# Two layers of graph network on 32 batches: where a search, a scaling, two norms and a verdict stand in the order

## The chip, the cores and the metric

The kernel runs on one core of a Trainium2 chip. The metric is the device time of one execution in microseconds (us), lower is better: 2764.36 us, the median of three runs from 2764.18 to 2764.61.

## What is computed

The reference, cut to what matters: 32 batches of 512 rows by 512 columns, one adjacency matrix of 512 x 512, all in float32.

```python
def layer0(x):                       # H = 8 heads of HD = 64
    q, k, v = x @ Wq + bq, x @ Wk + bk, x @ Wv + bv
    scores = einsum('bihd,bjhd->bhij', q, k) / sqrt(64)
    scores = scores + where(adj == 0, -1e9, 0)
    return einsum('bhij,bjhd->bihd', softmax(scores), v)

def layer1(x):
    y = einsum('nm,bmd->bnd', adj, x)
    return einsum('bnd,do->bno', y, weight) + bias

x = layernorm(x + layer0(x))
x = layernorm(x + layer1(x))
```

## The kernel before, in words

The work of a batch goes through TensorE in these steps. `project` (L372) makes q, k and v in seven products each instead of eight (a Strassen scheme over 2 x 2 blocks, `block_product` L362; the sums of blocks are made on VectorE and GpSimd). `scores` (L558) multiplies keys by queries per head, adds the mask on VectorE (L570), takes the exponential on ScalarE (L572) and adds up the exponentials on GpSimd (L583). `attend` (L585) multiplies by the values (L592). `fold_squares` (L614) and `add_up` (L628) make the sums of the softmax, and `turn_out` (L598) turns the result of a pair of heads by 32 x 32 blocks on VectorE and has SyncE copy 16 squares into `rows`, one DMA of 16 KB each (L611). `scale_rows` (L644) divides these rows by the sums on ScalarE (eight operations L649 for a pair of heads), and `add_rows` (L651) adds them to the input on GpSimd.

Then the first norm: `statistics` (L425) of four blocks of rows on VectorE (L431, L432), `square_root` (L434) on ScalarE, `invert_root` (L437, lines L440 and L441) on VectorE, `normalise` (L444, line L446) on ScalarE. For the second layer each row is split into a high half, rounded to TensorE's fast float format, and the rest: `split` (L464, lines L457 and L461). `aggregate` (L481) multiplies both halves by the adjacency matrix (L488), and `convolve` (L527) multiplies by the weight, again in seven products, whose results are added to the input on VectorE and, by way of a tile `mix`, on GpSimd (L537 to L544). The second norm is made with `statistics`, `norm` and `normalise` again (its statistics are called `survey`), and `store` (L468) writes a batch out.

The work is laid out by hand. [...] Units of work are listed by `units_of` (L722) for each batch, in two slots of the main loop (L764): slot 0 holds the projections of the next batch, slot 1 its values, the aggregation of the batch before and the convolution of the batch before. `merge` (L715) puts the lists named `behind` after the units of TensorE one by one. So in batch 31, the last, slot 0 holds the convolution of batch 29, with the statistics (`fresh`), root and norm (`young`) and the splits of batch 30 behind its products, and slot 1 the aggregation of batch 30.

What follows the main loop is the end of the last batch (L786 to L844), in which nothing of a later batch is left to fill TensorE's waits: the convolution of batch 30 (`rest`), the first norm of batch 31, its aggregation by rows (`split_rows` L497, lines L502 and L503; `add_bias` L505; `aggregate_rows` L508, products L515, copies to `yT` L520 and L522), its convolution (`last`), and the second norms of batches 29, 30 and 31 with their stores. In the aggregation by rows the high and low tiles have two buffers each, so the third block's halves wait for the first block's products, and the fourth's for the second's.

The kernel takes two shortcuts that hold for the given kind of input, and tests them as it goes: that sums of exponentials stay finite, and whether the adjacency matrix is exact in the fast format. For the second, `look_for_low_half` (L305) rounds a block of rows on ScalarE (L308), compares it with the original on VectorE into a tile of the tag `attT` (L310), and counts the differences (L311). The tag has two buffers, which `turn_out` uses as well. `judge` (L665) makes one number per row of all tests, in seven small operations of VectorE; a last product of TensorE (L843) adds them up, and VectorE writes `verdict` (L844). After it every engine reads the verdict and branches: were it 1, a general kernel would run.

Results of TensorE lie in a ring of eight banks (`bank`, L223); a new product waits until the bank's reader of eight products ago is done.

Of the kernel before, what the change touches and what calls it, by code (L numbers as in the profile page):

```python
# [207 lines left out]
def fast_kernel(ctx: ExitStack, tc, verdict, x, adj, Wq, bq, Wk, bk, Wv, bv, W1, b1, out):  # L208
# [3 lines left out]
    HP = H // 2  # L212
    NB = N // P
    DB = D // P
    assert N == 512 and D == 512 and H * HD == D
    root = float(HD) ** 0.5

    consts = ctx.enter_context(tc.tile_pool(name="consts", bufs=1))
# [249 lines left out]
    def store(b, blocks=None):  # L468
        for c in blocks or ():
            nc.sync.dma_start(out[b, c * P:(c + 1) * P, :], X[b][:, c, :])  # L470
        if blocks is None:
            nc.sync.dma_start(out[b].rearrange("(c p) d -> p c d", p=P), X[b])
# [30 lines left out]
        nc.vector.tensor_sub(low, row, high.bitcast(FP))  # L503

    def add_bias(b, c):  # L505
        nc.vector.tensor_add(X[b][:, c, :], X[b][:, c, :], b1_r)  # L506

    def aggregate_rows(b):  # L508

        yt = YT[b] = work.tile([P, 7, 2, half], FP, name="yT", bufs=1)  # L510
        banks = [bank(2, half) for _ in range(DB)]
        for c in range(NB):
            for d, pm in enumerate(banks):
                for part in (LOW[b, c], HIGH[b, c]):
                    nc.tensor.matmul(pm.rearrange("p a n -> p (a n)"), part[:, d * P:(d + 1) * P], adjT[:, c, :],  # L515
                                     start=(c == 0 and part is LOW[b, c]), stop=(c == NB - 1 and part is HIGH[b, c]))
        for d, pm in enumerate(banks):
            block = yt[:, d // 2:d // 2 + 3:2, d % 2, :]
            if d % 2:
                nc.vector.tensor_copy(block, pm)  # L520
            else:
                nc.scalar.activation(block, pm, AF.Copy)  # L522
            if d >= 2:
                nc.vector.tensor_add(yt[:, A_AT["S1"], d % 2, :], pm[:, 1, :], yt[:, A_AT["A21"], d % 2, :])
        combine_rows(yt)

    def convolve(b, i):  # L527

        pm = bank(2, half)
        block_product(pm, YT[b], w1, i)  # L530
        x11, x12, x21, x22 = (X[b][:, 2 * r:2 * r + 2, s * half:(s + 1) * half] for r in range(2) for s in range(2))
        if i == 1:

            MIX[b] = work.tile([P, 2, half], FP, name="mix", tag="q" if b >= B - 3 else "low", bufs=2)
            nc.scalar.activation(MIX[b], pm, AF.Copy)
        if i in (6, 7):
            nc.vector.tensor_add(MIX[b], pm, MIX[b])  # L537
            for block in (x12,) if i == 6 else (x21, x22) if b == B - 1 else (x22,):
                nc.gpsimd.tensor_add(block, block, MIX[b])
        for block in {1: (x11,), 5: (x12, x22), 2: (x11,), 3: (x12,), 4: (x21,)}.get(i, ()):  # L540
            nc.vector.tensor_add(block, pm, block)  # L541
        if i == 4 and b < B - 1:

            nc.gpsimd.tensor_add(x21, x21, MIX[b])  # L544
# [6 lines left out]
    def convolution(b):  # L551
        return [(convolve, b, i) for i in (1, 2, 5, 6, 7, 3, 4)] if b >= 0 else []
# [125 lines left out]
    def run(units):  # L678
        for unit in units:
            unit[0](*unit[1:])  # L680
# [26 lines left out]
    def survey(b):  # L707

        return [(statistics, b, 1, c) for c in range(NB)] if b >= 0 else []
# [5 lines left out]
    def merge(units, behind):  # L715

        merged = []
        for k in range(max(len(units), len(behind))):
            merged += units[k:k + 1] + (behind[k] if k < len(behind) else [])
        return merged  # L720

    def units_of(b):  # L722

        made, turned = projections(b + 1), flips(b + 2)
        splits, gathered = aggregation(b - 1)
        old, seen = norm(b - 1, 1), survey(b - 2)

        fresh, young = ([(statistics, b - 1, 0, c) for c in range(NB)], norm(b - 1, 0)) if b else ([], [])
        scaled, added = residuals(b, 0)
        if b == B - 1:  # L730


            first, second = folds(b, 1)
            behind = [fresh[:2], fresh[2:], young[:1], young[1:3], young[3:5] + [first], young[5:] + splits[:1],
                      splits[1:]]
            return [merge(convolution(b - 2), behind), [second] + merge(gathered, [scaled, added, seen[:2], seen[2:]])]

        ready = [(turn_over, b)] if b > 1 else []
        if old:
            behind = [seen[:2], seen[2:], old[:2], old[2:4] + fresh[:2], old[4:] + ready + fresh[2:]] + [  # L740
                [u] for u in young]
        elif b:
            behind = [ready + fresh] + [[u] for u in young]
        else:
            behind = [[]] + [[(sum_weights, w1, n)] for n in range(4)]
        behind += [[] for _ in range(11 - len(behind))]
        behind += [splits[:1], scaled + added, splits[1:2]]
        slot0 = merge(made[:16], behind)
        values = made[16:]
        looked = [(look_for_low_half, c) for c in range(NB)] if b == 0 else []  # L750
        scaled, added = residuals(b, 1)
        slot1 = values[:3] + looked[:2] + gathered[:1] + splits[2:3] + gathered[1:2] + splits[3:] + scaled[:1]
        slot1 += values[3:] + looked[2:]
        if b == B - 2 > 0:
            slot1 += [(load, B - 1)]
        slot1 += gathered[2:3] + turned[:1] + gathered[3:]
        convolved = convolution(b - 1) if b < B - 2 else []
        slot1 += merge(convolved, [scaled[1:] + added[:1] + turned[1:2], turned[2:3], turned[3:4], [], [], [],
                                   added[1:] + turned[4:]])
        return [slot0, slot1]  # L760
# [27 lines left out]
    rest, last = convolution(t - 1), convolution(t)  # L788
    for hp in range(HP - PAIRS, HP):
        last_residual(t, hp)  # L790
    run(rest[:1])
    old, seen = norm(t - 1, 1), survey(t - 1)
    run(old[:1] + rest[1:2] + old[1:])
    if t > 1:
        store(t - 2)

    for c in range(NB):
        statistics(t, 0, c)
    ahead = norm(t, 0)
    run(ahead[:1] + rest[2:3] + ahead[1:2])  # L800
    for c in range(NB):
        run(ahead[2 + c:3 + c] + rest[3 + c:4 + c])
        split_rows(t, c)
    run(rest[3 + NB:])
    for c in range(NB):
        add_bias(t, c)
    aggregate_rows(t)


    halves = {}  # L810
# [4 lines left out]
            halves[c] = spare[:, c, :, :]  # L815
        nc.vector.bn_stats(halves[c][:, s, :], X[t][:, c, s * half:(s + 1) * half])  # L816

    old = norm(t, 1)
    beside = {1: seen, 2: old[:2], 5: old[2:3], 6: old[3:5], 7: old[5:]}
    for unit in last:  # L820
        run([unit] + beside.get(unit[2], []))
        if unit[2] == 2:
            well = judge()
        if unit[2] == 7 and t > 0:
            store(t - 1)
        for c, s in {2: ((0, 0), (1, 0)), 3: ((0, 1), (1, 1)), 4: ((2, 1), (3, 1), (2, 0), (3, 0))}.get(unit[2], ()):
            half_statistics(c, s)
            if (c < 2) == (s == 1):
                if t + 1 not in STAT:
                    for table, name, shape in ((STAT, "stat", (2 * NB, 2)), (RSTD, "rstd", (2 * NB,)),  # L830
                                               (SHIFT, "shift", (2 * NB,))):
                        table[t + 1] = work.tile([P, *shape], FP, name=name, bufs=3)
                nc.vector.bn_aggr(STAT[t + 1][:, NB + c, :], halves[c])
        ready = {3: (0, 1), 4: (2, 3)}.get(unit[2], ())
        if ready:
            slots = slice(NB + ready[0], NB + ready[1] + 1)
            square_root(t + 1, slots)
            invert_root(t + 1, slots)
            for c in ready:
                normalise(t + 1, NB + c)  # L840
                store(t, [c])
    pm = bank(N)
    nc.tensor.matmul(pm[0:1, 0:1], well, ones[:, 0:1], start=True, stop=True)  # L843
    nc.vector.tensor_scalar(verdict, pm[0:1, 0:1], P - 0.5, None, op0=ALU.is_lt)  # L844


# [22 lines left out]
```

## Time and profile before

| | |
|---|---|
| median of three runs | 2764.36 us |
| the profiled execution | 2764.78 us |
| its span, first to last instruction | 2762.9 us |
| TensorE, busy in the span | 2735.6 us, 99% |
| VectorE | 2068.2 us, 75% |
| GpSimd | 1902.6 us, 69% |
| ScalarE | 1411.1 us, 51% |
| last product of TensorE ends | 2749.9 us after the span's start |
| last store is issued | 2757.6 us |

The page names engines PE (TensorE), PEld (its weight loads), DVE (VectorE), ACT (ScalarE), POOL (GpSimd) and SP (SyncE, whose DMA issues are shown as SPq). L570 is line 570 of the kernel. A line of the waits reads: engine, line, who released it, us in total, how many times, the longest. A line of the timeline reads: start in us from the span's start, how long the group took, engine, line, operation, output <- input with sizes, count, and in brackets the engine's idle time before it and what ended that. One matmul in float32 shows as two passes, so x8 are four products. A product of 128 x 128 by 128 x 512 halves (L488, L515) is one pass.

From batch 2 on the main loop repeats every 84.9 us, TensorE without a wait.

### The profile page before, as it was taken

The page shows a single profiled execution, that of the slowest core. Times are in us where ns is not written, and L with a number is a line of the kernel's source. Part 1 is how long each engine was busy: PE and PEld are TensorE (multiplying, and loading weights), DVE is VectorE, ACT ScalarE, POOL GpSimd, SP SyncE. Part 2 cuts the span into 40 slices and gives each one's busy share as a digit, 9 for nine tenths or more (in the row PEclk, how much of TensorE's full clock was granted, in tenths as well). Part 3 has the DMA queues.
Part 4 walks back from the last instruction along what each step waited for, and adds up shares of the span by engine and source line. Part 5 has one row for each costly group of instructions (what it writes and reads, how often), then busy time and mean ns, then how long its engine had stood idle before and what let it go on. Part 6 is the DMA issues. An engine that isn't in the chain of part 4 may idle for free.

```text
span 2762.9 us, 39328 instructions
## 1 busy us (share of the span) xinstructions
PE 2735.6 (99%) x12842; PEld 1912.7 (69%) x12842; DVE 2068.2 (75%) x3347; ACT 1411.1 (51%) x2459; POOL 1902.6 (69%) x1223
## 2 busy tenths in 40 slices
PE   9999999999999999999999999999999999999997
PEld 6666766767767667677676676776766767767665
DVE  6777777787777777777777777777777777787777
ACT  2455544655545546445554465454554544655554
POOL 4666777667767667676677776776666867667774
PEclk9999999999999999999999999999999999999999
DMA  5122212222122222122221222211222212222121
GB/s 147 29 31 57 45 30 56 60 60 56 25 49 58 61 56 36 38 56 62 58 53 21 56 59 60 56 26 48 58 62 57 44 30 56 61 58 57 26 51 49
DMA packets 592915, 142.20 MB, mean 51 GB/s; under 512 B 554560, under 2 KB 558656, under 8 KB 592704
## 3 DMA queue, kind: packets, MB, share of 16 engines
q1 hardware_dynamic: 592704, 139.63, 23.1%
q8 instruction: 103, 1.69, 0.3%
q14 instruction: 108, 0.88, 0.1%
HBM read 72.88 MB, written 33.55 MB: 39 GB/s over the span
## 4 chain that ended last, share of the span: by engine, by line
PE 97%; DVE 1%; SPq 1%; ACT 0%; DMA 0%; issue 0%; POOL 0%; DVEq 0%; ACTq 0%
PE bank L369 55%; PE bank L568 16%; PE bank L592 16%; PE bank L488 8%; SPq L611 1%; PE bank L633 0%; DVE bnst L431 0%; DMA wq<-in_L_gnn_Wq_dram 0%; ACT rows L649 0%; PE bank L515 0%; DVE xT L541 0%; DVE part L816 0%; DVE xs L541 0%; DVE xT L506 0%; DVE low L503 0%
## 5 line engine op out<-in xcount | busy, mean ns | idle before, releaser
L572 ACT ACTIVATE e<-e 128x1024 f32<-128x1024 f32 x512 | 524.6, 1053 | 581.3 <-DVE e L570 559.5
L570 DVE SCALAR_TENSOR_TENSOR e<-gap,bank 128x512 f32<-128x512 uint8 x1024 | 617.9, 681 | 20.2 <-PE bank L568 20.2
L583 POOL TENSOR_TENSOR es<-es,e 128x1024 f32<-128x1024 f32 x256 | 618.2, 2415 | 20.1
L583 POOL TENSOR_TENSOR es<-e 128x1024 f32<-128x1024 f32 x128 | 315.9, 2468 | 333.0 <-ACT e L572 333.0
L568 PE MATMUL bank<-q,k 64*128 64x512 f32 x2048 | 465.2, 599 | 0.0
L592 PE MATMUL bank<-e,v 128*64 128x512 f32 x2048 | 456.5, 598 | 4.7 <-DVE v L404 4.7
L369 PE MATMUL bank<-wv,xT 128*128 128x256 f32 x1792 | 405.4, 381 | 0.0
L369 PE MATMUL bank<-xT,wk 128*128 128x256 f32 x1792 | 403.0, 379 | 0.7 <-DVE wk L319 0.7
L369 PE MATMUL bank<-xT,wq 128*128 128x256 f32 x1792 | 403.1, 383 | 0.4 <-DMA wq<-in_L_gnn_Wq_dram 0.4
L369 PE MATMUL bank<-w,yT 128*128 128x256 f32 x1792 | 392.3, 379 | 0.5 <-DVE yT L520 0.5
L568 PEld LDWEIGHTS bank<-q,k 64*128 64x128 f32 x2048 | 204.0, 186 | 259.6 <-issue 160.4
L369 PEld LDWEIGHTS bank<-w,yT 128*128 128x128 f32 x1792 | 340.0, 190 | 48.1 <-DVE yT L520 0.9
L369 PEld LDWEIGHTS bank<-xT,wk 128*128 128x128 f32 x1792 | 340.2, 190 | 47.2 <-PE bank L369 1.1
L369 PEld LDWEIGHTS bank<-xT,wq 128*128 128x128 f32 x1792 | 339.5, 191 | 47.4 <-ACT xT L344 0.8
L369 PEld LDWEIGHTS bank<-wv,xT 128*128 128x128 f32 x1792 | 337.5, 190 | 47.5 <-DVE e L570 0.8
L649 ACT ACTIVATE rows<-rows,zero,inverse 128x64 f32<-128x64 f32 x1008 | 343.2, 427 | 0.0
L592 PEld LDWEIGHTS bank<-e,v 128*64 128x64 f32 x2048 | 142.2, 137 | 283.8 <-issue 282.7
L653 POOL TENSOR_TENSOR xs<-xs,rows 128x512 f32<-128x512 f32 x124 | 158.4, 1289 | 168.0 <-DMA xs<-in_x_dram 168.0
L572 ACT ACT_TABLE_LOAD x30 | 38.5, 1283 | 423.9 <-DVE e L570 423.9
L461 DVE TENSOR_TENSOR low<-xs,high 128x512 fp32r<-128x512 f32 x122 | 143.5, 1176 | 104.2 <-ACT high L457 104.2
L446 ACT ACTIVATE xs<-xs,shift,rstd 128x512 f32<-128x512 f32 x248 | 181.9, 803 | 32.5 <-DVE shift L441 32.5
L541 DVE TENSOR_TENSOR xs<-bank,xs 128x512 f32<-128x512 f32 x186 | 124.5, 683 | 96.9 <-PE bank L369 46.5
(122 smaller groups left out, 2970.1 us busy)
## 6 DMA issues: line engine op xcount, KB each, us to landing
rows<-attT SPq DMA_DIRECT2D x2016, 16.0 KB, 1.8
xin<-in_x_dram SPq DMA_DIRECT2D x496, 64.0 KB, 2.5
xs<-in_x_dram SPq DMA_DIRECT2D x31, 1024.0 KB, 5.2
out_dram<-xs SPq DMA_DIRECT2D x31, 1024.0 KB, 4.4
xin<-in_x_dram SPq DMA_DIRECT2D x4, 256.0 KB, 3.6
wq<-in_L_gnn_Wq_dram SPq DMA_DIRECT2D x2, 512.0 KB, 6.2
wk<-in_L_gnn_Wk_dram SPq DMA_DIRECT2D x2, 512.0 KB, 8.2
yT<-in_adj_dram SPq DMA_DIRECT2D x1, 1024.0 KB, 7.9
```

The lines of the kernel that those rows point to most:

```text
L369: nc.tensor.matmul(pm[:, r, :], left[:, d, r * P:(r + 1) * P], right[:, d, :], start=(d == 0), stop=(d == 1))
L446: nc.scalar.activation(row, row, AF.Identity, bias=SHIFT[t][:, slot:slot + 1], scale=RSTD[t][:, slot:slot + 1])
L461: nc.vector.tensor_sub(LOW[b, d], cols, HIGH[b, d].bitcast(FP))
L488: nc.tensor.matmul(pm.rearrange("p a n -> p (a n)"), part, adjT[:, n % NB, :], start=(n == 0), stop=(n == 2 * NB - 1))
L541: nc.vector.tensor_add(block, pm, block)
L568: nc.tensor.matmul(ps[s], keys[:, j * P:(j + 1) * P], queries, start=True, stop=True)
L570: nc.vector.scalar_tensor_tensor(e[:, s, :], gap[:, j, :], NEG * root, ps[s], op0=ALU.mult, op1=ALU.add)
L572: nc.scalar.activation(e, e, AF.Exp, scale=1.0 / root)
L583: nc.gpsimd.tensor_add(ES[b, hp], ES[b, hp] if j > 1 else E[b, hp, 0], E[b, hp, j])
L592: nc.tensor.matmul(po[s * HD:(s + 1) * HD, :], values, e[:, s, :], start=(j == 0), stop=(j == NB - 1))
L649: nc.scalar.activation(part, part, AF.Identity, bias=zero, scale=inverse[:, c, s:s + 1])
L653: nc.gpsimd.tensor_add(cols, cols, ROWS.pop((b, hp)))
```

## The change

It moves steps and changes a few; the products of TensorE stay the same and in the same order, the verdict's excepted.

- The four searches (`look_for_low_half`) leave slot 1 of batch 0 and stand behind the eighth to eleventh products of slot 0 of batch 1.
- Slot 0 of batch 31: `scaled`, the scaling of the first two pairs of heads, stands behind the first two products of batch 29's convolution, ahead of the root of batch 30's norm; before, it stood behind the first two aggregations of slot 1. The statistics of batch 29 (`seen`) leave slot 1.
- At the end: the norm of batch 29 and the statistics of batch 30 leave the convolution of batch 30. Statistics of batch 29 and two of batch 30 are now made between that convolution's last addition and `aggregate_rows`, and the rest beside the last convolution, with both norms and stores.
- `add_bias` of batch 31 runs on GpSimd instead of VectorE.
- In the last convolution the seventh product's sum goes to a new `mix` tile instead of the one that GpSimd reads.
- `judge` stands behind the fourth product (unit 6) of the last convolution, and the verdict's product behind the fifth (unit 7), ahead of the last two; before, it was the last.
- The last norm: blocks 2 and 3 take their statistics after blocks 0 and 1 are normalised, and block 3 is normalised on VectorE.

```diff
-        nc.vector.tensor_add(X[b][:, c, :], X[b][:, c, :], b1_r)
+        nc.gpsimd.tensor_add(X[b][:, c, :], X[b][:, c, :], b1_r)
...
-            nc.vector.tensor_add(MIX[b], pm, MIX[b])
+            mixed = MIX[b]
+            if i == 7 and b == B - 1:
+                MIX[b] = work.tile([P, 2, half], FP, name="mix", tag="q", bufs=2)
+            nc.vector.tensor_add(MIX[b], pm, mixed)
...
-            behind = [fresh[:2], fresh[2:], young[:1], young[1:3], young[3:5] + [first], young[5:] + splits[:1],
-                      splits[1:]]
-            return [merge(convolution(b - 2), behind), [second] + merge(gathered, [scaled, added, seen[:2], seen[2:]])]
+            behind = [fresh[:2] + scaled[:1], fresh[2:] + scaled[1:], young[:1], young[1:3], young[3:5] + [first],
+                      young[5:] + splits[:1], splits[1:]]
+            return [merge(convolution(b - 2), behind), [second] + added + gathered]
...
             behind = [ready + fresh] + [[u] for u in young]
+            behind += [[(look_for_low_half, c)] for c in range(NB)]
...
-        looked = [(look_for_low_half, c) for c in range(NB)] if b == 0 else []
...
-        slot1 = values[:3] + looked[:2] + gathered[:1] + splits[2:3] + gathered[1:2] + splits[3:] + scaled[:1]
-        slot1 += values[3:] + looked[2:]
+        slot1 = values[:3] + gathered[:1] + splits[2:3] + gathered[1:2] + splits[3:] + scaled[:1]
+        slot1 += values[3:]
...
     run(rest[:1])
-    old, seen = norm(t - 1, 1), survey(t - 1)
-    run(old[:1] + rest[1:2] + old[1:])
-    if t > 1:
-        store(t - 2)
-
     for c in range(NB):
         statistics(t, 0, c)
     ahead = norm(t, 0)
-    run(ahead[:1] + rest[2:3] + ahead[1:2])
+    run(ahead[:1] + rest[1:2] + ahead[1:2])
     for c in range(NB):
-        run(ahead[2 + c:3 + c] + rest[3 + c:4 + c])
+        run(ahead[2 + c:3 + c])
         split_rows(t, c)
-    run(rest[3 + NB:])
+        run(rest[2 + c:3 + c])
+    run(rest[2 + NB:])
+    older, seen = survey(t - 2), survey(t - 1)
+    run(older)
     for c in range(NB):
         add_bias(t, c)
+    run(seen[:2])
     aggregate_rows(t)
+    old = norm(t - 1, 1)
...
-    old = norm(t, 1)
-    beside = {1: seen, 2: old[:2], 5: old[2:3], 6: old[3:5], 7: old[5:]}
+    next_ = norm(t, 1)
+    beside = {1: old + seen[2:3], 2: seen[3:] + next_[:2], 5: next_[2:4], 6: next_[4:]}
+    upper, lower = slice(NB, NB + 2), slice(NB + 2, 2 * NB)
     for unit in last:
         run([unit] + beside.get(unit[2], []))
+        if unit[2] == 1 and t > 1:
+            store(t - 2)
         if unit[2] == 2:
+            for c in range(2):
+                half_statistics(c, 0)
+        if unit[2] == 6:
             well = judge()
-        if unit[2] == 7 and t > 0:
-            store(t - 1)
...
+            if t > 0:
+                store(t - 1)
+        if unit[2] == 3:
+            for c in range(2):
+                half_statistics(c, 1)
+                close(c)
+            square_root(t + 1, upper)
+        if unit[2] == 7:
+            pm = bank(N)
+            nc.tensor.matmul(pm[0:1, 0:1], well, ones[:, 0:1], start=True, stop=True)
+            nc.vector.tensor_scalar(verdict, pm[0:1, 0:1], P - 0.5, None, op0=ALU.is_lt)
+    invert_root(t + 1, upper)
+    for c in range(2):
+        normalise(t + 1, NB + c)
+        store(t, [c])
+    for c in (2, 3):
+        half_statistics(c, 1)
+        half_statistics(c, 0)
+        close(c)
+    square_root(t + 1, lower)
+    invert_root(t + 1, lower)
+    normalise(t + 1, NB + 2)
+    row = X[t][:, 3, :]
+    nc.vector.tensor_scalar(row, row, STAT[t + 1][:, NB + 3, 0:1], RSTD[t + 1][:, NB + 3:NB + 4],
+                            op0=ALU.subtract, op1=ALU.mult)
+    store(t, [2, 3])
```

`half_statistics` (L813) takes the statistics of half a block's columns, `close` joins the two halves of a block. The order of the last products is 1, 2, 5, 6, 7, 3, 4.

More of the change, by code (lines that the diff above doesn't have):

```diff
@@ L214, in fast_kernel @@
     DB = D // P
-    assert N == 512 and D == 512 and H * HD == D
+    assert N == 512 and D == 512 and H * HD == D and B > 2
     root = float(HD) ** 0.5
@@ L816, in half_statistics, with close @@
         nc.vector.bn_stats(halves[c][:, s, :], X[t][:, c, s * half:(s + 1) * half])
-    old = norm(t, 1)
-    beside = {1: seen, 2: old[:2], 5: old[2:3], 6: old[3:5], 7: old[5:]}
+    def close(c):
+        nc.vector.bn_aggr(STAT[t + 1][:, NB + c, :], halves[c])
+    for table, name, shape in ((STAT, "stat", (2 * NB, 2)), (RSTD, "rstd", (2 * NB,)), (SHIFT, "shift", (2 * NB,))):
+        table[t + 1] = work.tile([P, *shape], FP, name=name, bufs=3)
+    next_ = norm(t, 1)
+    beside = {1: old + seen[2:3], 2: seen[3:] + next_[:2], 5: next_[2:4], 6: next_[4:]}
@@ L820, in fast_kernel @@
+    upper, lower = slice(NB, NB + 2), slice(NB + 2, 2 * NB)
     for unit in last:
         run([unit] + beside.get(unit[2], []))
+        if unit[2] == 1 and t > 1:
+            store(t - 2)
         if unit[2] == 2:
+            for c in range(2):
+                half_statistics(c, 0)
+        if unit[2] == 6:
             well = judge()
-        if unit[2] == 7 and t > 0:
-            store(t - 1)
[L826 to L844, printed above, removed]
+            if t > 0:
+                store(t - 1)
```

## The prediction

> **What bounds the kernel now.** I read the page first, then TensorE's waits, then the timeline of each engine where TensorE idles: early in batch 1, and in the last batch.
>
> ```profile
> span 2762.9 us, 39328 instructions
> PE 2735.6 (99%) x12842; PEld 1912.7 (69%) x12842; DVE 2068.2 (75%) x3347; ACT 1411.1 (51%) x2459; POOL 1902.6 (69%) x1223
> ```
>
> TensorE is the bound. Only its idle time, its slow clock and the tail behind its last product can change; the change leaves its products alone. The waits:
>
> ```profile
> PE bank L592 <- DVE v L404: 4.7, 1, 4.7
> PE bank L515 <- DVE low L503: 4.3, 2, 4.0
> ...
> PE bank L369 <- DVE yT L520: 0.5, 1, 0.5
> ```
>
> The change touches all three. TensorE around the first (start, duration):
>
> ```profile
> 124.40 1.94 PE L592 MATMUL bank<-e,v 128*64 128x512 f32 x8
> 131.02 8.03 PE L592 MATMUL bank<-e,v 128*64 128x512 f32 x24 [4.68 <-DVE v L404]
> 138.98 9.47 PE L568 MATMUL bank<-q,k 64*128 64x512 f32 x32
> ```
>
> VectorE in the same stretch: a search stands in a DMA wait, and the values behind it are late:
>
> ```profile
> 127.80 1.15 DVE L310 TENSOR_TENSOR attT<-yT,high 128x512 f32<-128x512 f32 x1 [4.54 <-DMA rows<-attT]
> 128.99 0.69 DVE L311 TENSOR_REDUCE inexact<-attT 128x1 f32<-128x512 f32 x1
> 129.59 1.28 DVE L404 TENSOR_TENSOR v<-bank,v 128x512 f32<-128x512 f32 x2
> 142.44 9.62 DVE L570 SCALAR_TENSOR_TENSOR e<-gap,bank 128x512 f32<-128x512 uint8 x16
> ```
>
> GpSimd meanwhile adds up the exponentials that the second fold of this stretch needs:
>
> ```profile
> 126.06 5.10 POOL L583 TENSOR_TENSOR es<-es,e 128x1024 f32<-128x1024 f32 x2
> ```
>
> In the last batch, the lines of TensorE, ScalarE and SyncE that I price from:
>
> ```profile
> 2702.58 1.20 PE L488 MATMUL bank<-adjT,low 128*128 128x512 f32 x4
> 2727.58 0.76 PE L515 MATMUL bank<-adjT,low 128*128 128x512 f32 x1 [3.96 <-DVE low L503]
> 2738.07 11.92 PE L369 MATMUL bank<-w,yT 128*128 128x256 f32 x54 [0.46 <-DVE yT L520]
> ```
> ```profile
> 2692.96 0.30 ACT L435 ACTIVATE rstd<-stat,eps 128x4 f32<-128x4 f32 x1 [3.26 <-DVE stat L432]
> 2695.49 2.93 ACT L446 ACTIVATE xs<-xs,shift,rstd 128x512 f32<-128x512 f32 x4 [2.24 <-DVE shift L441]
> 2705.24 5.42 ACT L649 ACTIVATE rows<-rows,zero,inverse 128x64 f32<-128x64 f32 x16
> ```
> ```profile
> 2676.78 21.50 SPq L611 DMA_DIRECT2D rows<-attT  x32
> ```
>
> [...] granted clock 0.50 from 131 to 136 us and from 2727.5 to 2730.5. There 24 passes took 7.96 instead of 24 x 0.2193 = 5.26 (2.7 lost), and 24 of L515 took 7.16 instead of 24 x 0.2325 (1.6 lost). [...] L503 took 0.69 alone and 1.38 beside POOL's L544.
>
> **Part 1, the searches moved to batch 1.** Removed from batch 0: four pairs L310+L311, 6.6 us (1.6+1.8+1.6+1.7, start to start), and the 4.5 us DMA wait. Without them L404 follows its last product (124.4) and ends near 125.1. Four transposes L353 take 2.4 (127.5), fold and turn of the first head pair (L623, L625, L606: 136.43 to 139.43 before) 3.0 to 3.1 (130.6). The second fold needs GpSimd's sums, done at 131.16: so 131.2, and with 3.05 its turn ends at 134.25. Then L570 starts, at 142.44 before: 8.2 earlier. Before, too, VectorE paced those scores (9.47 against 7.14 us elsewhere), so what follows on TensorE moves by the same **8.2**. Bounds: 9.9, all that this stretch loses (from one run of 128 products L369 to the next 75.18 us, where the pieces of the chain, 27.8 + 2 x (7.02 + 7.14 + 0.2) for attention and 5 x 1.74 for five value products, give 65.2), and 7.0, if the sums come a microsecond late. In the new place VectorE idles 10.4 us between 157.5 and 177.5 and gets 6.6 more; the rows that free the two attT buffers should have landed by then (estimate 155.3, search 157). ScalarE's four copies, 2.2 us, and the scaling behind them come some 6 us late, into idle time ahead of the second half of the batch. Cost 0; 1 to 2 if that cover is short. Batch 0 has no DMA of its own in this edit, and SyncE's queue keeps its order.
>
> **Part 2, scaling of the last batch in front of the square root.** Sixteen L649 now stand behind the mix (ends 2688.4), ahead of table load, L435 and L446. Their rows are issued one by one by SyncE: 32 from 2676.78, the last at 2697.7, landing 1.8 us later: 2699.5. The first eight end near 2691.4; of the second pair all but the first operation wait for the last rows: 2699.55 + 2.42 = 2702.0. In the order of the changed program the table load still stands directly before the root, so it can no longer run early. Then table 1.28, root 0.30 (2703.6), L440 and L441 (2704.0), four L446 2.93 (2707.0), L457 0.6 (2707.6), L461 0.7 (2708.3): L488 starts at 2708.4 instead of 2702.58. The change adds a wait: behind it on ScalarE stand root, norm and high halves of batch 30, on VectorE L440 and everything after, on TensorE the aggregation. **5.8** idle, plus 1.6 of slow clock (0 to 2.8): **7.4**. The 5.4 us freed later on ScalarE hide behind the aggregation.
>
> **Part 3, statistics and norm of batches 29 and 30 moved back.** Let T be the end of that aggregation. VectorE reaches the first residual product L660 at T+1.3, 4.6 us earlier against T than before, without four statistics in front. With residuals 2.7, add 0.6, own statistics 3.3, root and shift 1.0, L446 0.8, L502 0.6, L503 0.7 the first low half is there at T+11. The product itself comes free later: TensorE is done at T+13.4 (8 transposes and 12.25 of L369). The L515 wait goes: 3.96 + 1.6 + 0.3 = **-5.9**. What is late next: the yT copy. Between the last L503 and L520 now stand two adds (1.2), four statistics of batch 29 and two of batch 30 (6 x 0.8 = 4.8); the four bias adds (2.4) have gone to GpSimd, 4 x 1.27 there, done before TensorE needs them. With S the start of L515: the last L503 must wait for the second block's products, S+3.7, high half, and GpSimd's add beside it: ends S+5.75. Then 1.2, 4.8 and the copy 0.6: S+12.4. L515 ends at S+7.75, half a product follows: idle 4.15 instead of 0.46, and 0.3 for the last block: **+4.0**; slow clock +0.75 (0 to 2.8)[...].
>
> The stores of batches 29 and 30 also go later on SyncE, behind norms that end near S+19 and S+22; a store of 1 MB lands in 4.3 us, so both are out before the last four are issued (S+28 on). Cost 0.
>
> **Part 4, judge and verdict.** VectorE's order in the last products is: first add (behind the mix), L440, statistics, add, statistics, L440 (waiting for ScalarE's four L446), half statistics, two adds, mix, seven small operations 0.8. From S+12.4: yT copies and sums 1.3 beside the first product (S+14.1), mix copy 0.6, add 0.6, L440 and L441 0.4, statistics 0.8, add 0.6, statistics 0.8, then the wait until the root behind four L446 is there (S+19.0), 0.4, half statistics 0.7, adds 1.2, mix 0.6, judge 0.8. That gives S+22.8; TensorE has its first five products at S+20.8. The verdict product stands between, so it waits **+1.9** (0 to 2).
>
> **Part 5, the end.** Now 2762.9 - 2749.9 = 13.0 follow the last product: VectorE lags, since L537 stood 1.38 us behind GpSimd (the new mix tile ends this). New, from the last product's end: add 0.75, inverse and shift 0.35, statistics of blocks 2 and 3 1.85, root 0.35, inverse 0.4, L446 0.85 with block 3 on VectorE beside it, second store's issue 0.4, then 5.3 as now from the last issue to the end: 10.3. **-2.7** (-2 to -3.3).
>
> **Sum.** -8.2 + 7.4 - 5.9 + 4.0 + 0.75 + 1.9 - 2.7 = -2.75. The profiled run took 2764.78 (span 2762.9 and 1.9 around it): 2762.0. The median is 0.42 lower: **2761.6**. What a measurement can tell is 0.2%, 5.5 us: faster below 2758.8, slower above 2769.9.
>
> **Rivals.** *The rows come in time* (0.12): then part 2 costs nothing and the total is -10.2: 2754.2. For it: in batches before, the same scaling found its rows landed. Against: SyncE's 21.5 us of issue, which begins when GpSimd frees the rows' buffers at 2676.7 and which the change doesn't touch. *The searches take their price along* (0.07), the slower side: if in batch 1 the rows land later than the search, VectorE stands before it, behind it the eviction of projections. As soon as eight banks (8 x 1.74 us) don't cover the delay, TensorE waits; with the whole 8.2 back, the tail's +5.45 stays: 2769.9, and with both slow clocks at their upper ends 2773. Against: the 10.4 idle. *Slow clock and verdict at their lower ends* is inside my case: -2.75 - 1.6 - 0.75 - 1.9 = -7, 2757.4; both clocks at their upper ends give 2764.9.
>
> **How the numbers follow.** Forecast 0.81, of it 0.12 under 2758.8; rivals 0.12 and 0.07. Faster 0.24, same 0.69, slower 0.07. The forecast's own range is 2757 to 2766.5 with the bounds of parts 1 to 5; the rivals' 0.19 may stay outside.
>
> **What would show it.** Part 1: no L592 wait, batch 1's first L369 near 140.3. Part 2: L488 waits about 6 us on L461, ScalarE idle before L649. Part 3: no long L515 wait, about 4 us on L520. Part 4: a 1 to 2 us wait at the verdict. Wrong would be: scaling without a wait, or a search that waits on DMA again.

## The result, and the profile after

The changed kernel takes 2766.02 us (median of 12 runs, 2763.67 to 2767.72), the kernel before 2764.57 us (12 runs beside it, 2763.43 to 2765.93). The ratio is 1.0005, 95% interval 0.9997 to 1.0012: no difference that can be told. The forecast of 2761.6 us was 4.4 us too low. In the traces the span grew from 2762.9 to 2764.7 us, by 1.8, where the sum had said -2.75. So there are 4.55 us to find.

The page of the kernel after, its first lines (TensorE's busy time counts slow passes as busy, 5.20 of 5.20 us at a granted clock of 0.50 further down, so it says nothing about the clock):

```profile
span 2764.7 us, 39351 instructions
PE 2735.4 (99%) x12842; PEld 1915.2 (69%) x12842; DVE 2065.1 (75%) x3344; ACT 1411.5 (51%) x2458; POOL 1908.4 (69%) x1227
```

TensorE's waits of the kernel after. The L592 wait (now L596) is gone and the one of L515 is down to 0.3, as meant; three others stand there instead:

```profile
PE bank L488 <- DVE low L461: 5.7, 1, 5.7
PE bank L369 <- DVE yT L520: 4.0, 1, 4.0
PE bank L849 <- DVE well L678: 2.8, 1, 2.8
PE bank L515 <- DVE low L503: 0.3, 1, 0.3
```

TensorE at the start of batch 1, kernel after. The 32 passes of values run through, and the first projection of the batch starts at 139.42 instead of 148.57:

```profile
124.03 7.09 PE L596 MATMUL bank<-e,v 128*64 128x512 f32 x32
131.05 8.26 PE L572 MATMUL bank<-q,k 64*128 64x512 f32 x32
139.42 8.90 PE L369 MATMUL bank<-xT,wq 128*128 128x256 f32 x40
```

TensorE at the end, kernel after. In front of each of the three groups stands its wait, in brackets. Read the durations too: 38 passes that take 8.47 at full speed took 10.16, and the last 16 took 5.40 instead of 3.72 (both full-speed values are from runs shown below):

```profile
2699.97 2.05 PE L488 MATMUL bank<-adjT,low 128*128 128x512 f32 x4 [5.71 <-DVE low L461]
2735.92 10.16 PE L369 MATMUL bank<-w,yT 128*128 128x256 f32 x38 [4.00 <-DVE yT L520]
2748.91 0.19 PE L849 MATMUL bank<-ones,well 128*1 128x1 f32 x2 [2.84 <-DVE well L678]
2749.04 5.40 PE L369 MATMUL bank<-w,yT 128*128 128x256 f32 x16
```

ScalarE in front of the first of these waits. The scaling (L653) waits for its rows, and table load and root stand behind it, as priced; the last statistics that the root needs were ready at 2684.53, and it ran at 2694.77:

```profile
2685.35 0.44 ACT L653 ACTIVATE rows<-rows,zero,inverse 128x64 f32<-128x64 f32 x1 [2.69 <-DMA rows<-attT]
2691.02 2.43 ACT L653 ACTIVATE rows<-rows,zero,inverse 128x64 f32<-128x64 f32 x7 [5.24 <-DMA rows<-attT]
2693.47 1.28 ACT L435 ACT_TABLE_LOAD   x1
2694.77 0.30 ACT L435 ACTIVATE rstd<-stat,eps 128x4 f32<-128x4 f32 x1
```

VectorE, kernel after, two lines that matter below: an idle stretch of 2.45 us in front of the third block's low half, and an operation of the judge on 128 x 2 numbers that took 1.18 us:

```profile
2726.09 0.69 DVE L503 TENSOR_TENSOR low<-xT,high 128x512 fp32r<-128x512 f32 x1 [2.45 <-ACT high L502]
...
2747.20 1.18 DVE L675 TENSOR_SCALAR well<-seen 128x2 f32<-128x2 f32 x1
```

GpSimd at that moment, kernel after, and the same operation of the judge in the kernel before (there L671):

```profile
2747.09 1.26 POOL L543 TENSOR_TENSOR xT<-xT,mix 128x512 f32<-128x512 f32 x1 [6.11 <-DVE mix L541]
```
```profile
2745.24 0.17 DVE L671 TENSOR_SCALAR well<-seen 128x2 f32<-128x2 f32 x1
```

The granted clock of TensorE, kernel after, in stretches behind the three waits (from:to, length, busy time of TensorE with its instructions, granted clock, share of the DMA engines, GB/s). Each wait is followed by a stretch at half speed:

```profile
2700.00:2705.20 5.20, 5.20 (x12) 0.50 0.00 0
2705.60:2707.00 1.40, 1.40 (x8) 1.00 0.00 0
2735.95:2736.15 0.20, 0.20 (x1) 1.00 0.00 0
2736.40:2739.40 3.00, 3.00 (x9) 0.50 0.00 0
2749.00:2749.70 0.70, 0.70 (x5) 1.00 1.03 389
2750.00:2753.10 3.10, 3.10 (x8) 0.50 0.44 161
```

Where the time went, step by step (after minus before, from the two timelines of TensorE; they add up to the 1.8 of the spans):

| step | predicted | in the traces |
|---|---|---|
| head: to batch 1's first projection | -8.2 | -9.15, of it 0.37 a lead from the first loads, ahead of anything that was changed |
| rest of the main loop | 0 | +0.8, of it 0.5 behind the searches |
| wait of L488 | +5.8 | +5.71 |
| its slow clock | +1.6 | +2.47 |
| aggregation's end to end of L515 | -5.9 | -5.55 |
| wait for the yT copy | +4.0 | +3.54 |
| its slow clock | +0.75 | +1.69 |
| wait for the verdict, with the product | +1.9 | +2.96 |
| its slow clock | not priced | +1.68 |
| last convolution in two pieces instead of one run | not priced | +0.33 |
| behind the last product | -2.7 | -2.71 |

The two later clock rows compare the same passes slow and at full speed (10.16 with 8.47, 5.40 with 3.72). The row of +0.33 is what is left: the two pieces at full speed take 12.19 us together, where the kernel before has one run of 11.92. Of the 4.55 us, 3.5 are slow clock (5.84 instead of 2.35), 1.06 is the verdict and 0.33 the two pieces; the other steps take back about 0.35.

### The profile page after: what moved, and what is told of

The parts are those of the page before. It is cut to its first block, busy times and chain, and to the rows that moved or that the text cites. A ratio compares the mean times of both kernels' runs of the same rounds, so it can differ in the third digit from the quotient of the medians.

```text
span 2764.7 us, 39351 instructions
## 1 busy us (share of the span) xinstructions
PE 2735.4 (99%) x12842; PEld 1915.2 (69%) x12842; DVE 2065.1 (75%) x3344; ACT 1411.5 (51%) x2458; POOL 1908.4 (69%) x1227
## 3 DMA queue, kind: packets, MB, share of 16 engines
q8 instruction: 103, 1.69, 0.2%
## 5 line engine op out<-in xcount | busy, mean ns | idle before, releaser
L596 PE MATMUL bank<-e,v 128*64 128x512 f32 x2048 | 453.6, 595 | 0.0
L369 PE MATMUL bank<-wv,xT 128*128 128x256 f32 x1792 | 405.4, 381 | 0.0
L369 PE MATMUL bank<-xT,wk 128*128 128x256 f32 x1792 | 403.0, 379 | 0.7 <-DVE wk L319 0.7
L369 PE MATMUL bank<-xT,wq 128*128 128x256 f32 x1792 | 402.1, 382 | 1.6 <-DMA wq<-in_L_gnn_Wq_dram 1.6
L369 PE MATMUL bank<-w,yT 128*128 128x256 f32 x1792 | 396.0, 381 | 4.0 <-DVE yT L520 4.0
L369 PEld LDWEIGHTS bank<-w,yT 128*128 128x128 f32 x1792 | 342.4, 191 | 52.6 <-DVE yT L520 4.4
L369 PEld LDWEIGHTS bank<-xT,wk 128*128 128x128 f32 x1792 | 340.2, 190 | 47.2 <-PE bank L369 1.1
L369 PEld LDWEIGHTS bank<-xT,wq 128*128 128x128 f32 x1792 | 338.9, 191 | 48.2 <-ACT xT L344 2.0
L369 PEld LDWEIGHTS bank<-wv,xT 128*128 128x128 f32 x1792 | 337.7, 190 | 47.4 <-DVE e L574 0.8
L653 ACT ACTIVATE rows<-rows,zero,inverse 128x64 f32<-128x64 f32 x1008 | 343.8, 428 | 13.2 <-DMA rows<-attT 13.2
L596 PEld LDWEIGHTS bank<-e,v 128*64 128x64 f32 x2048 | 141.4, 137 | 277.1 <-issue 276.5
```

What stands on the lines that cost most here:

```text
L369: nc.tensor.matmul(pm[:, r, :], left[:, d, r * P:(r + 1) * P], right[:, d, :], start=(d == 0), stop=(d == 1))
L596: nc.tensor.matmul(po[s * HD:(s + 1) * HD, :], values, e[:, s, :], start=(j == 0), stop=(j == NB - 1))
L653: nc.scalar.activation(part, part, AF.Identity, bias=zero, scale=inverse[:, c, s:s + 1])
```

## The experiments

The theory after the result: three waits on TensorE ate the gains of the head and of the L515 wait, and each is paid twice, once as idle time and once as slow clock behind it. Rivals: the waits cost no clock, and the long products behind them have another cause; or the end follows VectorE's queue, and a wait of TensorE is worth less than it shows. Each of the eight kernels ran in five rounds beside the kernel before, whose medians were 2764.92 (first four), 2764.74 (next three) and 2764.49 (last). Differences to after are against its median of 2766.02; since the median of the kernel before moved by up to 0.4 us between these groups of runs, they are good to about that.

**The searches alone** (the kernel before, with this edit only):

```diff
         elif b:
             behind = [ready + fresh] + [[u] for u in young]
+            behind += [[(look_for_low_half, c)] for c in range(NB)]
...
-        looked = [(look_for_low_half, c) for c in range(NB)] if b == 0 else []
...
-        slot1 = values[:3] + looked[:2] + gathered[:1] + splits[2:3] + gathered[1:2] + splits[3:] + scaled[:1]
-        slot1 += values[3:] + looked[2:]
+        slot1 = values[:3] + gathered[:1] + splits[2:3] + gathered[1:2] + splits[3:] + scaled[:1]
+        slot1 += values[3:]
```

> The kernel before with one part of the change alone: the four searches moved from batch 0 to batch 1. My theory, from the trace after (batch 1's first projection 8.8 us earlier, against a common start, and 0.5 us given back at the next scores): 8.0 to 8.6 us faster than before, about 2756.3. Rival, that the searches take their price along and the trace's gain is lost later in the main loop: no difference. Rival, that the tail reacts to the earlier start[...]: 4 to 6 us faster.

Measured: 2757.05 us (7 runs), ratio 0.9972 (0.9961 to 0.9983), 7.9 us under before, just short of the 8.0 to 8.6 expected. The gain of the head is real, and it reaches the end. The rival in which the searches take their price along falls. The long wait of L515 is still there in its trace, with thirteen passes at half speed behind it:

```profile
PE bank L515 <- DVE low L503: 4.0, 1, 4.0
```
```profile
2719.34 0.77 PE L515 MATMUL bank<-adjT,low 128*128 128x512 f32 x1 [3.98 <-DVE low L503]
...
2724.60 0.63 PE L515 MATMUL bank<-adjT,low 128*128 128x512 f32 x1
```

The kernel before has six such passes behind a wait of 3.96. The first 24 passes take 8.49 here and 7.16 there: the same wait cost 2.9 us of slow clock instead of 1.6. So the tail does react to the earlier start, as the second rival has it, but by losing time: TensorE is 8.3 us ahead of the kernel before when the last aggregation starts (2694.31 against 2702.58), and the span is 7.6 us shorter.

**The scaling alone** (the kernel before, with the scaling moved forward and nothing else):

```diff
-            behind = [fresh[:2], fresh[2:], young[:1], young[1:3], young[3:5] + [first], young[5:] + splits[:1],
-                      splits[1:]]
-            return [merge(convolution(b - 2), behind), [second] + merge(gathered, [scaled, added, seen[:2], seen[2:]])]
+            behind = [fresh[:2] + scaled[:1], fresh[2:] + scaled[1:], young[:1], young[1:3], young[3:5] + [first],
+                      young[5:] + splits[:1], splits[1:]]
+            return [merge(convolution(b - 2), behind), [second] + merge(gathered, [[], added, seen[:2], seen[2:]])]
```

> The kernel before with one part alone: the scaling of the last batch in front of batch 30's root; everything else of the tail as before. My theory: a wait of 5.7 us at the aggregation of batch 30 and about 2.5 us of slow clock, less up to 2 us at the later wait for the first low half, since the copies to yT no longer stand behind the scaling: 5.5 to 8 us slower than before, about 2771. Rival, that the scaling finds its rows landed or that the root is waiting for something else anyway: within 1 us of before.

Measured: 2768.89 us (21 runs), ratio 1.0014 (1.0008 to 1.0021), 4.0 us over before. The direction is right, the size was expected too large. Its timeline of TensorE shows why:

```profile
2708.93 2.04 PE L488 MATMUL bank<-adjT,low 128*128 128x512 f32 x4 [6.05 <-DVE low L461]
...
2733.27 0.48 PE L515 MATMUL bank<-adjT,low 128*128 128x512 f32 x1 [1.43 <-DVE low L503]
```

The price was 6.05 of waiting and 1.9 of clock (L488 took 9.54 instead of 7.67). But L515 now waits 1.43 instead of 3.96 us, and its 1.6 us of slow clock are gone: 4.1 us come back, twice what I had allowed. Where the shorter wait comes from can be read in the traces, and it is the reason that the expectation named. VectorE (L493) needs ScalarE's copy to `yT`, and in the kernel before sixteen scalings, 5.42 us, stand in front of that copy:

```profile
2711.65 0.42 DVE L493 TENSOR_TENSOR yT<-bank,yT 128x256 f32<-128x256 f32 x1 [2.98 <-ACT yT L491]
```
```profile
2717.34 0.42 DVE L493 TENSOR_TENSOR yT<-bank,yT 128x256 f32<-128x256 f32 x1 [0.84 <-ACT yT L491]
```

The first line is the kernel before, where L493 starts 1.40 us after the aggregation's end; the second is this run, where it starts 1.13 us before it. That is 2.53 us, all that the wait of L515 shrinks, since from L493 to the first low half (L503) both take 14.89 us.

**Scaling back behind the aggregation** (the kernel after, only this undone):

```diff
-            behind = [fresh[:2] + scaled[:1], fresh[2:] + scaled[1:], young[:1], young[1:3], young[3:5] + [first],
+            behind = [fresh[:2], fresh[2:], young[:1], young[1:3], young[3:5] + [first],
...
-            return [merge(convolution(b - 2), behind), [second] + added + gathered]
+            return [merge(convolution(b - 2), behind), [second] + merge(gathered, [scaled, added])]
```

> The changed kernel with one part undone: the scaling of the last batch behind the aggregation again. My theory: the wait at the aggregation and its slow clock go (5.7 + 2.5), the low half stays in time or comes up to 1 us late: 7 to 8.2 us faster than the changed kernel, about 2758.3. Rival, that ScalarE is then late with the copies to yT and the old wait at the row aggregation comes back in full (4 us and its slow clock): only 2 to 3 us faster.

Measured: 2758.54 us (9 runs), ratio to before 0.9976 (0.9966 to 0.9986), 7.5 us under after. In the changed kernel the move forward costs nearly all of its wait and clock (7.9 us of span against 8.2) and gives nothing back, since L515's wait is gone without it:

```profile
2694.46 1.20 PE L488 MATMUL bank<-adjT,low 128*128 128x512 f32 x4
...
2727.94 10.14 PE L369 MATMUL bank<-w,yT 128*128 128x256 f32 x38 [4.00 <-DVE yT L520]
```

**The waits filled with products** (the kernel after, with products whose result nobody reads, 20, 13 and 9 passes, in the three waits; the waits' ends stay where VectorE sets them). This separates idle time from clock:

```diff
+    def fill(n):
+        spare_bank = bank(N)
+        for _ in range(n):
+            nc.tensor.matmul(spare_bank, adjT[:, 0, 0:P], adjT[:, 0, :], start=True, stop=True)
...
-            return [merge(convolution(b - 2), behind), [second] + added + gathered]
+            return [merge(convolution(b - 2), behind), [(fill, 20), second] + added + gathered]
...
     aggregate_rows(t)
+    fill(13)
...
         if unit[2] == 7:
             pm = bank(N)
+            fill(9)
```

> The changed kernel with products added that nobody reads, 20, 13 and 9 passes, put into the three new waits of TensorE (before batch 30's aggregation, before the last convolution, before the verdict), a little shorter than the waits. The waits themselves stay, only the slow clock behind them should go. My theory, that slow clock is the term that I priced too low: 2.5 + 1.8 + 1.9 = 6.2 us, so 4.5 to 6.5 us faster than the changed kernel, about 2760.3, granted clock 1.0 behind all three. Rival, that these products are slow for another reason (memory beside GpSimd and DMA): no difference, or up to 1 us slower for the added work.

Measured: 2762.02 us (21 runs), ratio to before 0.9990 (0.9984 to 0.9997), 4.0 us under after; its profiled execution is 5.4 us shorter than after's. The median's gain is the smaller because after's profiled execution lies 0.6 over its median and this one's 0.8 under: a little less than expected, but a kernel with more work on TensorE ends earlier. Its timeline, behind the two later fills:

```profile
2733.59 8.47 PE L369 MATMUL bank<-w,yT 128*128 128x256 f32 x38 [1.01 <-DVE yT L520]
...
2745.41 3.72 PE L369 MATMUL bank<-w,yT 128*128 128x256 f32 x16
```

Where after has 10.16 and 5.40, it has 8.47 and 3.72: about 1.7 us each. The block of L488 takes 7.76 instead of 10.14. The slow clock is a price of its own, and it was paid behind the wait of 2.84 us too: the rival in which the products are slow for another reason falls, for the same passes run at full speed once the waits are filled.

**The verdict last again** (the kernel after, its product and read behind the last two products):

```diff
-        if unit[2] == 7:
-            pm = bank(N)
-            nc.tensor.matmul(pm[0:1, 0:1], well, ones[:, 0:1], start=True, stop=True)
-            nc.vector.tensor_scalar(verdict, pm[0:1, 0:1], P - 0.5, None, op0=ALU.is_lt)
...
+    pm = bank(N)
+    nc.tensor.matmul(pm[0:1, 0:1], well, ones[:, 0:1], start=True, stop=True)
+    nc.vector.tensor_scalar(verdict, pm[0:1, 0:1], P - 0.5, None, op0=ALU.is_lt)
```

> The changed kernel with the verdict's product and its reading moved behind the last two products; judge stays where the change put it. My theory: the wait of 2.8 us and the slow clock behind it (1.9) go, but then VectorE, which has no slack there, comes about 1.5 us late with the last additions: 3.0 to 3.6 us faster than the changed kernel, about 2762.7. Rival, that the end hangs on VectorE and ScalarE alone, so that TensorE's wait is covered: within 1 us of the changed kernel.

Measured: 2764.19 us (13 runs), ratio to before 0.9997 (0.9989 to 1.0006), 1.8 us under after: too much was expected. The wait went and the last of the 54 passes ended 4.3 us earlier, at 2750.18:

```profile
2736.57 13.61 PE L369 MATMUL bank<-w,yT 128*128 128x256 f32 x54 [4.00 <-DVE yT L520]
2750.11 0.19 PE L858 MATMUL bank<-ones,well 128*1 128x1 f32 x2
```

But 12.4 us followed it to the span's end, 2762.6, not 10.3: VectorE still makes the judge ahead of the last additions and is itself late. It leaves two readings of the verdict's wait: it is worth its idle time and clock, or only what VectorE's own lateness leaves. The run with the judge in the gap tells them apart.

**Three statistics in the gap** (the kernel after, three of batch 29's four statistics in VectorE's 2.45 us):

```diff
+    older, seen = survey(t - 2), survey(t - 1)
     for c in range(NB):
         run(ahead[2 + c:3 + c])
         split_rows(t, c)
         run(rest[2 + c:3 + c])
+        if c == 1:
+            run(older[:3])
     run(rest[2 + NB:])
-    older, seen = survey(t - 2), survey(t - 1)
-    run(older)
+    run(older[3:])
```

> The changed kernel with three of the four statistics of batch 29 put into the gap of 2.45 us in which VectorE waits for the third block's high half; the fourth and the two of batch 30 stay. My theory: the copy to yT comes 2.4 us earlier, the wait of 4.0 falls to 1.6, short enough that the clock stays up (1.8): 3.8 to 4.4 us faster than the changed kernel, about 2761.9. Rival, that the third low half is then late and the row aggregation waits instead: 0 to 2 us faster.

Measured: 2762.29 us (13 runs), ratio to before 0.9991 (0.9982 to 0.9999), 3.7 us under after, just short of the 3.8 to 4.4 expected. TensorE's timeline:

```profile
2733.39 8.47 PE L369 MATMUL bank<-w,yT 128*128 128x256 f32 x38 [1.62 <-DVE yT L520]
2744.69 0.19 PE L851 MATMUL bank<-ones,well 128*1 128x1 f32 x2 [2.83 <-DVE well L678]
2744.82 5.40 PE L369 MATMUL bank<-w,yT 128*128 128x256 f32 x16
```

A wait that shrinks from 4.00 to 1.62 us gives back 2.38 and the 1.69 of clock behind it (10.16 to 8.47). The verdict's wait stays, and its clock with it.

**The judge in the same gap** (the kernel after, its seven operations ahead of the third low half; product and read stay in front of the last products):

```diff
     for c in range(NB):
+        if c == 2:
+            well = judge()
         run(ahead[2 + c:3 + c])
...
         if unit[2] == 6:
-            well = judge()
             if t > 0:
                 store(t - 1)
```

> The kernel after with the seven small operations of the judge made ahead of the third block's low half, in VectorE's idle time of 2.45 us there; the verdict's product and its read stay in front of the last two products. Theory (a wait of 2.84 us is paid in full and lowers the clock behind it, and the end follows TensorE's last product): the verdict wait goes, and the last two products take 3.5 to 3.7 us instead of 5.40; the last product ends 4.5 to 5 us earlier and the end stays about 10.3 us behind it: 4.5 to 5 us faster than after, about 2761.3. Rival (as in the run with the verdict last, the end is set by VectorE's own queue, so most of the wait is given back behind the last product): 1.5 to 2.5 us faster, about 2764. Rival ([...]the 5.40 comes from something else): the wait's 2.8 us alone, about 2763.2, with the last two products still at 5.4.

Measured: 2762.41 us (13 runs), ratio to before 0.9994 (0.9985 to 1.0002), 3.6 us under after. That lies between the first two theories. TensorE's timeline decides: no wait, and full speed behind it:

```profile
2745.91 0.19 PE L850 MATMUL bank<-ones,well 128*1 128x1 f32 x2
2746.03 3.72 PE L369 MATMUL bank<-w,yT 128*128 128x256 f32 x16
```

The last product ends at 2749.75 instead of 2754.44, 4.7 us earlier, and 10.75 us follow instead of 10.26. So the wait with its clock is worth 4.7 on TensorE, and VectorE takes back half a microsecond of it in the trace. The profiled spans differ by 4.2, the medians by 3.6; the remaining 0.6 is less than the spread of either kernel's runs (2.9 and 4.05 us).

**A version that beats both** (the kernel after, with what the runs showed: the first pairs' scaling in front of the root, the second pairs' behind the first aggregation, three statistics in the gap, the judge ahead of the first low half with its product in front of the aggregation by rows, batch 30's statistics later):

```diff
-            behind = [fresh[:2] + scaled[:1], fresh[2:] + scaled[1:], young[:1], young[1:3], young[3:5] + [first],
+            behind = [fresh[:2] + scaled[:1], fresh[2:], young[:1], young[1:3], young[3:5] + [first],
...
-            return [merge(convolution(b - 2), behind), [second] + added + gathered]
+            return [merge(convolution(b - 2), behind), [second] + merge(gathered, [scaled[1:], added])]
...
+    older, seen = survey(t - 2), survey(t - 1)
     run(ahead[:1] + rest[1:2] + ahead[1:2])
+    well = judge()
     for c in range(NB):
...
+        if c == 1:
+            run(older[:3])
     run(rest[2 + NB:])
-    older, seen = survey(t - 2), survey(t - 1)
-    run(older)
+    run(older[3:])
     for c in range(NB):
         add_bias(t, c)
-    run(seen[:2])
+    pm = bank(N)
+    nc.tensor.matmul(pm[0:1, 0:1], well, ones[:, 0:1], start=True, stop=True)
+    nc.vector.tensor_scalar(verdict, pm[0:1, 0:1], P - 0.5, None, op0=ALU.is_lt)
     aggregate_rows(t)
...
-    beside = {1: old + seen[2:3], 2: seen[3:] + next_[:2], 5: next_[2:4], 6: next_[4:]}
+    beside = {1: old + seen[:1], 2: seen[1:3], 5: seen[3:] + next_[:2], 6: next_[2:4], 7: next_[4:]}
...
-        if unit[2] == 6:
-            well = judge()
+        if unit[2] == 7:
             if t > 0:
                 store(t - 1)
...
-        if unit[2] == 7:
-            pm = bank(N)
-            nc.tensor.matmul(pm[0:1, 0:1], well, ones[:, 0:1], start=True, stop=True)
-            nc.vector.tensor_scalar(verdict, pm[0:1, 0:1], P - 0.5, None, op0=ALU.is_lt)
```

> A version built from the findings: searches in batch 1, the first pair's scaling in front of the root (its rows have landed by then) and the second pair's behind the first aggregation as before, statistics of batch 29 in the gap, those of batch 30 beside the last convolution, judge in VectorE's wait before the first low half, the verdict's product before the row aggregation. My theory: none of TensorE's three new waits, none of the old ones in the tail, VectorE about 1.5 us late at the end: 2749 to 2751, 14 to 16 us faster than the kernel before. Rival, that VectorE is the bound of the last batch, so that whatever is taken from one wait comes back in another: 2756 or more, like the searches' move alone.

Measured: 2750.11 us (5 runs, 2749.87 to 2750.60), ratio to before 0.9948 (0.9934 to 0.9962): 14.6 us under before, 15.9 under after. The three single repairs add up to nearly that (7.5 + 3.7 + 3.6 = 14.8). What is left of the waits in its last batch:

```profile
PE bank L369 <- POOL yT L331: 1.1, 1, 1.1
...
PE bank L515 <- DVE low L503: 0.3, 1, 0.3
```

## Why the prediction was right and wrong

**Part 1, right.** -8.2 against -8.8 in the trace (the 9.15 less the lead of 0.37) and -7.9 in the run of the searches alone. "Cost 0; 1 to 2 if that cover is short" came out at 0.5: in batch 1 the fold (L627) began only at 169.93, and the scores beside it took 7.71 instead of 7.21 us.

**Part 2, right in kind.** 5.71 against 5.8 of waiting, through the chain named: last rows, scaling, table load, root, norm. The clock behind it was 2.47, not 1.6; the upper end of 2.8 covers it. The 1.6 is what the prediction reads off L515 in the kernel before, where the clock was low from 2727.1 to 2730.5; here it was low from 2698.6 to 2705.5, the last 5.5 us with work. The rival in which the rows come in time falls. Undoing the move alone gains 7.5: in the changed kernel it costs nearly its whole wait and clock. The sentence that the time freed later on ScalarE hides behind the aggregation holds there; in the kernel before it was worth 2.53 us of wait, as the run of the scaling alone shows.

**Part 3, right in the waits, wrong in the clock.** -5.55 against -5.9, and L369 waits 4.00 us for the yT copy, where 4.15 was named. The step that failed is "slow clock +0.75 (0 to 2.8)". That is half of the 1.6 that the kernel before shows behind its wait of 3.96; the half was my estimate, and no trace showed it. Measured: 1.69, which is gone when the wait is filled or cut to 1.62 us.

**Part 4, the wait too small and its clock left out.** 2.84 against +1.9 (0 to 2). About one microsecond is L675, 1.18 instead of the 0.17 of before: GpSimd's L543 ran from 2747.09 to 2748.35, and L675, begun at 2747.20, ended at 2748.38. The run with three statistics in the gap confirms that it isn't the slow clock in front: the passes there ran at full speed, L675 again took 1.18, and the wait was 2.83. In the best version it ran with GpSimd idle and took 0.17. To the wait came 1.68 of slow clock, which the prediction put at nothing and gave no reason; that the wait would cost no clock was my estimate, for on TensorE the kernel before has no wait between 0.73 and 3.71 us that could show it.

**Part 5, right.** -2.71 against -2.7.

So the mechanisms of the waits were the right ones, and the terms of the clock were mis-sized, all in one direction. In parts 3 and 4 the reason is the same: I priced waits of 4.15 and 1.9 us by estimates that no trace showed, and both were too low. Measured in the last batch: 2.83 to 2.86 us of waiting were followed by slow clock in three traces (after, scaling back, statistics in the gap: 5.40 us for the sixteen passes that take 3.72 at full speed), and none of the waits of 0.3 to 1.6 us was. The clock's 3.5, the verdict's 1.06 and the 0.33 of the two pieces are 4.9, against 4.55 that the sum was short; the other terms take back the difference.

That the measured time lies inside the forecast's own range of 2757 to 2766.5 is in part luck: it is half a microsecond from the upper end, and part 4 alone, 4.6 with its clock against 0 to 2, left its bounds. In the rivals' sums, 2764.36 + 5.45 is 2769.8, not 2769.9. The sign of the change itself, +1.45 us in the medians, is not told from zero.

## What to carry to other kernels

In the tail of a kernel, price a wait of TensorE twice: its idle time, and the slow clock behind it, in these traces 1.6 to 2.9 us behind waits of 2.83 to 6.05 us. Moving work forward on an engine pays only if its inputs are there: sixteen small scalings in front of a root cost the arrival of the last rows, here a wait of 5.71 us. Ask, too, what the work held up where it stood before: there, the same scalings kept back the copies to `yT`, which was worth 2.53 us. Look for the idle stretches of the late engine itself (here 2.45 us between two low halves) and put the displaced work there.

## What was not expected of the hardware

**The clock's steps.** In after's trace the changes of the granted clock lie 3.41 us apart or multiples of it: down near 2698.6, up again near 2705.5 (2 times 3.41 later), down near 2736.2 (9 times), up near 2739.6, down near 2749.8 (3 times), up near 2753.2. Twice the fall came when work had already resumed: at 2735.92, slow from about 2736.2, and at 2748.91, slow from about 2749.8. In the 3.41 us ahead of that second fall TensorE was busy from 2748.91 on, 27% of them. And the first 3.41 us at half clock (2698.6 to 2702.0, work from 2699.97) were 60% busy, and the clock stayed at 0.50 behind them; the next 3.41 us were busy throughout, and behind them it was back at 1.00. In the kernel before it stayed low behind 3.41 us that were 58% busy (129.6 to 133.0, behind the wait of L592) and came back behind 3.41 us that were 87% busy (2727.1 to 2730.5, behind the wait of L515).

The wait in front of L515 is almost the same in the run of the searches alone, 3.98 us, and in the kernel before, 3.96. The passes behind it were slow from 2719.34 to about 2725.1 in the one, 5.8 us, and from 2727.58 to about 2730.5 in the other, 2.9 us. So it was not the wait's length alone that made it cost 2.9 us of slow clock or 1.6. What decides each step, these traces don't show.

Nor do they show how far a wait's price differs from one execution to the next, since each kernel has one trace, and the spread of the runs doesn't settle it: it is 4.05 us over 12 runs of after and 0.7 over 5 of the best version, but also 3.7 over 21 runs of the filled waits, whose longest wait in the tail is 1.14 us, and only 1.9 over 9 with the scaling back, which keeps waits of 4.00 and 2.86.

**A small operation of VectorE that ended with GpSimd's addition.** What the tiny L675 took beside GpSimd doesn't follow its size. It took 1.18 to 1.22 us in five traces (after, scaling back, verdict last, statistics in the gap, judge in the gap), beside an L543 each time, and ended 0.03 us behind that L543 in all five. Without one it took 0.17, in the kernel before (there L671) and in the best version. A second case in after's trace is L441, on 128 x 4 numbers: it began at 2740.19 beside GpSimd's L333 and took 0.81 instead of 0.16 us; it ended at 2741.00, L333 at 2740.99. L440 just before it, beside the same addition, took its usual 0.17. Why the one took longer there and the other did not, these traces don't show.
